# Moving the bound, mirror, statistics and row-number pieces of the even attention steps in a graph-network kernel's tick plan

## The chip, the core and the metric

The kernel runs on one core of a Trainium2 chip. The metric is device time in microseconds (us) of one execution. Three runs of the kernel before gave 1163.94, 1170.53 and 1171.4 us, median 1170.53. One more execution was recorded by the hardware profiler and took 1240.64 us.

The engines are written PE (TensorE, matmuls), DVE (VectorE), ACT (ScalarE), POOL (GpSimd) and SP (SyncE, which issues transfers). Each works through its own list of instructions, and semaphores hold an instruction until what it needs is there.

## What is computed

Sixteen graphs of 1024 nodes with 128 features each, and a 0/1 adjacency matrix per graph. Layer 0 is masked attention, layer 1 a three-stage graph convolution on a thinned ("dilated") adjacency:

```python
h = jnp.maximum(_layernorm(x, axis=-1), 0.0)
# layer 0
v = relu(h @ Wv.T + bv); q = relu(h @ Wq.T + bq); k = relu(h @ Wk.T + bk)
att = softmax((q @ k.T) * mask - NEG * (1.0 - mask))
x = x + relu((att @ v) @ Wo.T + bo)
h = jnp.maximum(_layernorm(x, axis=-1), 0.0)
# layer 1: the pattern is thinned row by row; earlier rows' removals count
def step(carry, n):
    row = carry[n]; num = row.sum()
    sf = where(num > 10, (num + 1) // 2, 1)
    rm = row & (cumsum(row) % sf == 0) & (num > 1)
    carry[n] = row & ~rm; carry[:, n] &= ~rm
adj_d = adj * dilate(adj)
# three times: agg = adj_d @ h / deg; h = bn(relu(normalize(agg @ Wr + h @ Wx + b)))
# then x + concat(h1, h2, h3) @ Wl + bl
```

The adjacency is sparse enough that most rows cannot lose a neighbour. The kernel therefore finds the few rows that can (the "bound"), sorts them, gathers their rows, solves the thinning for them alone, and checks that the input is of the kind that allows this (0/1 entries, symmetric).

## The kernel before

`fast` runs three stages. The first is attention, one step per graph: `step(i)` for i = 0 to 15, and it is there that the change lies. The graph convolution follows in the later part of the program (three passes, with batch norms between them).

**A step and its ticks.** A step has 16 blocks of scores: two groups of 512 queries by eight blocks k of 128 keys. In each block, `scores` issues one matmul of 128 x 512 (L731), whose exponential (ACT, L733) and product with the mask (DVE, L734) are queued one and two ticks later. After that come twice two matmuls of `values` (L747) for the group before. The function `pace` is called three times in a block, once after the scores and once after each half of the values; each call is one **tick**. A step thus has 48 ticks. Everything else that has to be done beside attention is written as generators which yield between pieces, and a plan says at which tick of a step each generator is advanced. Ticks over 47 fall into the next step. Each piece is put on its engines' lists at its tick, in the order of the agenda, so the plan fixes the order of instructions on each engine.

**The pieces that the change touches**, for step i:

- `bound(i)` (`AT_BOUND`), 17 pieces. Piece 0 is `prepare`: the upper triangles of the diagonal blocks `du` (DVE, L210) and two limits (L211, L213). Then for each of eight blocks of rows k two pieces: matmuls into a PSUM buffer `pd` (k times L237 on the comparisons `away` of the blocks before, then one L238 on `du`), and a DVE comparison L240 that reads the `pd` and writes `away[k]`. Block k + 1 needs the comparison of block k.
- `mirrors(i)` (`AT_MIRRORS`), 8 pieces. Piece k transposes k + 1 blocks of the adjacency on PE into a `pd` (L193), and one tick later DVE compares them with the rows (L199).
- `project(i + 1)` (`AT_PROJECT`), the next graph's q, k and v. Its first five pieces are the layer norm's statistics: four DVE statistics (L590), then the last one, with a DVE negation (L593) and a chain of 14 small POOL instructions (L597 to L603). Four pieces of normalising on POOL (L609, which writes `hn`), two of PE transposes (L619) and the matmuls (L710, L718) follow.
- `gather(b)` (`AT_GATHER`), for the two graphs b of a pair, planned in odd steps; many of its ticks are over 47, so they run in the next even step. Its pieces: four of DVE one-hots (L295); PE row numbers into a `pd` (L300); a DVE instruction that reads them (L303); an indirect DMA on POOL (L306) that fetches the rows; a DVE scan over them (L310); the codes (DVE, L313); PE transposes into a `pd` (L317); two ACT evictions (L321); PE matmuls into a `pd` (L325); and DVE reads of these (L328, L330, L331). The buffers `rows` and `left` exist once, so the second graph's L306 waits for the first graph's L313.
- `norms_of_x2(i - 1)` (`AT_NORMS`), the statistics of the finished rows in the same form; its last piece is followed by `store(i - 1)` (eight indirect DMAs from POOL, L565) from tick 75.

All these `pd` are turns of one PSUM buffer name with two buffers; so a matmul of a later piece waits until DVE or ACT has read the piece two turns earlier. In PSUM, the scores have two buffers (`ps`), the values two (`po`), the projection one (`pm`), and the solver one (`pb`).

**The solver.** In steps 5 to 7, 9 to 12 and 13 to 15, `solve` is spread over the ticks as well: small DVE instructions, pairs of DVE masks (L367) and PE matmuls (L399, L400) that need both masks.

**The scheduling is by hand.** The order in the lists is the order in which the code issues; nothing is moved later. In the plan, the first entry of each pair of lists is for even steps and the second for odd ones, except in `AT_GATHER`, where the first is for the pair's even graph and the second for its odd graph. In step 0 every tick t becomes 24 + t // 2.

```python
plan(dil.bound(i), start, late(AT_BOUND[odd]))
plan(dil.mirrors(i), start, late(AT_MIRRORS[odd]))
if i + 1 < B:
    plan(project(i + 1), start, late(AT_PROJECT[odd]))
```

## Time and profile before

| | us |
|---|---|
| median of three runs (1163.94 to 1171.4) | 1170.53 |
| the profiled execution | 1240.64 |
| its span, first to last instruction | 1238.8 |
| its stretch from the start of step 1 to that of step 15 (72.4 to 735.2) | 662.8 |
| mean granted PE clock over the span | 0.946 |

The profile has, for each engine, how long it was busy and in which instructions, named by line, tile and shape; what an engine waited for before an instruction ("idle before <- releaser"); a chain of waits that leads to the last instruction; and tables by stretch of the span, with the clock that was granted to PE. A line of the timeline reads: start in us, duration in us, engine, line, operation, output <- inputs, shape, count, and in brackets the idle time before it with what ended it. Matmul ends in it are modelled, so that neighbouring matmuls overlap by some tenths of a microsecond.

The costliest attention groups, and the DVE groups that stand around the bound:

| group | busy, us | mean of one, ns | idle before |
|---|---|---|---|
| PE L747, values, x2048 | 315.3 | 289 | 0.0 |
| PE L731, scores, x512 | 272.4 | 616 | 0.8 |
| DVE L734, mask product, x256 | 177.9 | 695 | 162.4, mostly for ACT's exponential |
| ACT L733, exponential, x256 | 153.1 | 598 | 120.4, mostly for the scores |
| DVE L310, scan, x16 (median of one) | | 2283 | |
| DVE L313, codes, x16 (median of one) | | 1218 | |
| DVE L590, statistics, x128 (median of one) | | 418 | |
| DVE L240, the bound's comparison, x128 (median of one) | | 152 | |

### The profile page before, as it was taken

How to read it: one execution, taken by the hardware profiler on the slowest of the kernel's cores; microseconds unless marked ns; L12 is line 12 of the kernel's file. 1: busy time of each engine (PE TensorE's matmuls, PEld its weight loads, DVE VectorE, ACT ScalarE, POOL GpSimd, SP SyncE). 2: the span in 40 equal slices, each digit the busy share in tenths (PEclk: the TensorE clock that was granted, in tenths of full speed). 3: DMA queues.
4: the chain of work that ended last, by engine and by line, in shares of the span. 5: the costliest groups of instructions: out<-in, count | busy, mean ns of one | idle time of the engine just before them, and what ended most of it. 6: DMA issues, size and time to landing. Idle time of an engine off the chain costs nothing.

```text
span 1238.8 us, 22489 instructions
## 1 busy us (share of the span) xinstructions
PE 1077.9 (87%) x7731; PEld 832.2 (67%) x7731; DVE 850.6 (69%) x2611; ACT 736.8 (59%) x1772; POOL 566.4 (46%) x1071
## 2 busy tenths in 40 slices
PE   7899998997998999899999898687879988788675
PEld 2566676665676676676666666576769977778565
DVE  6667567578677667777777778678878866555432
ACT  5577787876776777776776652276757722222211
POOL 0220642651733643643634514678601037767552
PEclk8899999999899999999999899999989989889698
DMA  6444345344344344344343321334010037667534
GB/s 210 140 133 137 104 137 153 102 125 148 90 120 135 113 126 144 104 129 137 112 128 90 121 65 37 90 90 119 1 35 1 2 89 224 208 199 205 160 118 129
DMA packets 138589, 145.89 MB, mean 118 GB/s; under 512 B 25952, under 2 KB 114400, under 8 KB 138464
## 3 DMA queue, kind: packets, MB, share of 16 engines
q1 hardware_dynamic: 126432, 112.68, 32.1%
q0 software_dynamic: 12032, 31.67, 7.7%
q8 instruction: 63, 1.03, 0.4%
q14 instruction: 62, 0.51, 0.1%
HBM read 114.76 MB, written 29.56 MB: 116 GB/s over the span
## 4 chain that ended last, share of the span: by engine, by line
PE 59%; DVE 19%; ACT 8%; POOL 4%; issue 4%; another core or an unknown queue 3%; DMA 1%; SPq 0%; DVEq 0%; POOLq 0%; ACTq 0%
PE po L747 13%; PE ps L731 13%; PE pm L710 6%; PE po L1019 5%; DVE e L734 3%; PE pd L193 3%; PE pt L1077 2%; ACT e L733 2%; PE ph L1359 2%; PE ph L1297 2%; POOL hn L609 2%; PE ph L1298 2%; DVE left L310 2%; PE pm L718 1%
## 5 line engine op out<-in xcount | busy, mean ns | idle before, releaser
L747 PEld LDWEIGHTS po<-vw,e 128*128 128x128 f32 x2048 | 278.3, 198 | 62.7 <-issue 62.3
L747 PE MATMUL po<-vw,e 128*128 128x129 f32 x2048 | 315.3, 289 | 0.0
L734 DVE TENSOR_TENSOR e<-e,ab 128x512 f32<-128x512 f32 x256 | 177.9, 695 | 162.4 <-ACT e L733 145.1
L731 PE MATMUL ps<-qT,kT 128*128 128x512 f32 x512 | 272.4, 616 | 0.8 <-ACT e L733 0.8
L733 ACT ACTIVATE e<-ps 128x512 f32<-128x512 f32 x256 | 153.1, 598 | 120.4 <-PE ps L731 86.3
L565 POOL DMA_INDIRECT x_d<-xt,slot x128 | 142.8, 1115 | 40.4 <-issue 33.2
L167 ACT ACTIVATE ab<-st,d_one_k 128x1024 bf16<-128x1024 f32 x128 | 147.1, 1149 | 2.5 <-DMA st<-in_adj_dram 2.4
L184 ACT ACTIVATE junk<-st 128x1024 bf16<-128x1024 f32 x112 | 118.1, 1054 | 0.0
L565 POOL DMA_INDIRECT y_d<-y,nodes x96 | 94.2, 982 | 23.7 <-issue 20.3
L597 POOL TENSOR_SCALAR ln_t<-ln_st 128x8 f32<-128x8 f32 x31 | 7.5, 242 | 207.2 <-DVE ln_st L590 193.2
L306 POOL DMA_INDIRECT rows<-in_adj_dram,row x16 | 18.0, 1124 | 179.5 <-DVE row L303 98.5
L1035 ACT ACTIVATE sq<-po 128x512 f32<-128x512 f32 x48 | 28.6, 598 | 99.9 <-remote 44.7
L731 PEld LDWEIGHTS ps<-qT,kT 128*128 128x128 f32 x512 | 79.5, 195 | 6.6 <-ACT e L733 2.8
L756 ACT ACTIVATE o<-po,recips 128x128 f32<-128x128 f32 x128 | 46.7, 367 | 55.2 <-DVE recips L754 42.7
L1019 PE MATMUL po<-ws,r 128*128 128x128 f32 x512 | 69.9, 280 | 3.3 <-issue 3.3
L1019 PEld LDWEIGHTS po<-ws,r 128*128 128x128 f32 x512 | 66.8, 197 | 5.2 <-issue 4.0
L199 DVE SCALAR_TENSOR_TENSOR junkv<-pd,ab 128x64 bf16<-128x64 int32 (+7 forms) x128 | 57.8, 451 | 17.2 <-PE pd L193 12.3
L609 POOL TENSOR_SCALAR hn<-xt,ln 128x128 f32<-128x128 f32 x120 | 68.8, 588 | 1.6
L1297 PE MATMUL ph<-ws,r 128*128 128x128 f32 x224 | 49.0, 301 | 16.3 <-DVE y L1094 6.2
L609 POOL TENSOR_SCALAR hn<-xt 128x128 f32<-128x128 f32 x112 | 56.3, 516 | 12.7 <-PE pt L619 11.9
L237 PEld LDWEIGHTS <-ab 128*128 128x128 bf16 x448 | 26.6, 98 | 49.7 <-issue 49.4
L1032 ACT ACTIVATE sq<-po 128x128 f32<-128x128 f32 x192 | 51.0, 292 | 10.4 <-PE po L1026 5.7
(341 smaller groups left out, 2439.3 us busy)
## 6 DMA issues: line engine op xcount, KB each, us to landing
st<-in_adj_dram SPq DMA_DIRECT2D x128, 512.0 KB
r<-y_d SPq DMA_DIRECT2D x24, 512.0 KB
xt<-x_d SPq DMA_DIRECT2D x16, 524.0 KB
xt<-in_x_dram SPq DMA_DIRECT2D x16, 512.0 KB
x<-x_d SPq DMA_DIRECT2D x16, 512.0 KB
out_dram<-r SPq DMA_DIRECT2D x12, 512.0 KB
x_d<-xt,slot POOLq DMA_INDIRECT x128
y_d<-y,nodes POOLq DMA_INDIRECT x96
```

The source lines that it names most:

```text
L167: nc.scalar.activation(ab[:, k, :], st, AF.Exp, bias=self.one_k, scale=ONE_K, accum_out=self.deg[:, b, k:k + 1])
L184: nc.scalar.activation(junk(), st, AF.Exp, scale=-ZERO_K, accum_out=zeros)
L199: nc.vector.scalar_tensor_tensor(junk.rearrange("p a b -> p (a b)")[:, :n], pt.rearrange("p a b -> p (a b)").bitcast(I32)[:, :n], 1.0, ab[ ...
L565: d = nc.gpsimd.indirect_dma_start(out=dst, out_offset=bass.IndirectOffsetOnAxis(ap=slots, axis=0), in_=src, in_offset=None)
L609: engine.tensor_scalar(hn[:, k, :], xt[:, k, :D], minus[:, k // 2, k % 2, None], rstd[:, k // 2, k % 2, None], op0=OP.add, op1=OP.mult)
L710: nc.tensor.matmul(pp, w, hT[:, 512 * g:512 * g + 512], start=True, stop=True)
L731: nc.tensor.matmul(p, K[b][:, k * P:(k + 1) * P], Q[b][:, c], start=True, stop=True)
L733: later(1, lambda: nc.scalar.activation(e, p, AF.Exp))
L734: later(2, lambda: nc.vector.tensor_mul(e, e, AB_[b][:, k, c]))
L747: nc.tensor.matmul(po[:, q % 2, :], E[k][:, i * P:(i + 1) * P], V[b][:, k, :], start=(k == 0), stop=(k == NB - 1))
L1019: nc.tensor.matmul(po[:, i, :], hT[:, c:c + P], wxk, start=(i == 3), stop=False)
L1297: nc.tensor.matmul(pz[:, i, :], column(r1, b, g, i), wl0, start=True, stop=False)
```

## The change

Only numbers of the plan change, and with them the order of instructions. In even steps, the bound's two pieces for block k move from ticks 9 + 3k and 10 + 3k to ticks 2 + 5k and 3 + 5k. The mirrors move to 5, 10, 20, 25, 30, 35, 40 and 44. The projection's statistics are taken at ticks 1, 2, 4 and 7 instead of 1, 7, 11 and 12; its fifth piece stays at 13. The odd graph's row numbers (matmul L300 and DVE's L303), which run in the next even step, move from its ticks 6 and 7 to 3 and 4; the even graph's scan stays at tick 7 of that step and its codes at tick 10. Of the norms, the first statistics of even steps moves from 30 to 27; of those planned in odd steps that fall into the next even step, the third statistics moves from tick 10 of it to tick 17, and the last piece from 22 to 24. Odd steps keep the ticks of what runs in them.

```diff
         AT_PROJECT = [m + every(m[4] + 4, 4, 1) + every(m[4] + 12, 10, 3)
-                      for m in ([1, 7, 11, 12, 13], [0, 1, 3, 5, 6])]
+                      for m in ([1, 2, 4, 7, 13], [0, 1, 3, 5, 6])]
         AT_LOAD = every(1, 2 * NB, 3)
-        AT_BOUND = [[0] + [first + 3 * (j // 2) + j % 2 for j in range(2 * NB)] for first in (9, 3)]
-        AT_MIRRORS = ([20, 23, 29, 33, 35, 39, 42, 44], [13, 16, 19, 22, 25, 29, 33, 41])
+        AT_BOUND = [[0] + [first + by * (j // 2) + j % 2 for j in range(2 * NB)] for first, by in ((2, 5), (3, 3))]
+        AT_MIRRORS = ([5, 10, 20, 25, 30, 35, 40, 44], [13, 16, 19, 22, 25, 29, 33, 41])
 
         AT_SORT = [27, 29, 31, 32, 33, 35, 36]
         AT_GATHER = ([37, 38, 39, 40, 43, 44, 47, 55, 58, 63, 64, 65, 69, 70],
-                     [41, 43, 46, 49, 54, 55, 61, 81, 85, 89, 90, 91, 93, 94])
+                     [41, 43, 46, 49, 51, 52, 61, 81, 85, 89, 90, 91, 93, 94])
         LAST_GATHER = [37, 38, 39, 40, 43, 44, 46, 50, 54]
-        AT_NORMS = ([30, 57, 67, 68, 71], [42, 44, 58, 67, 70])
+        AT_NORMS = ([27, 57, 67, 68, 71], [42, 44, 65, 67, 72])
         AT_STORE = every(75, NB, 2)
```

## The prediction

> **What bounds the kernel now.** I read the page's busy shares first, then the chain of waits, then the attention steps one by one, then the queues around the longest wait of a step. On the page TensorE (PE) has most work and the chain runs mainly over it:

> ```profile
> PE 1077.9 (87%) x7731; PEld 832.2 (67%) x7731; DVE 850.6 (69%) x2611; ACT 736.8 (59%) x1772; POOL 566.4 (46%) x1071
> ...
> PE 59%; DVE 19%; ACT 8%; POOL 4%; issue 4%; another core or an unknown queue 3%; DMA 1%; SPq 0%; DVEq 0%; POOLq 0%; ACTq 0%
> ```

> A step begins where VectorE (DVE) builds the upper triangles (L210). These are the even steps 2, 4, 6, 8, 10, 12 and 14 in a table by stretches: the stretch, its length, PE busy, granted clock.

> ```profile
> 115.20:160.70 45.50, 43.09 (x293) 0.96 0.43 138
> 205.20:250.20 45.00, 42.02 (x295) 1.00 0.45 128
> 299.30:349.90 50.60, 44.93 (x317) 0.93 0.39 118
> 398.30:444.00 45.70, 43.28 (x293) 0.96 0.44 133
> 491.30:536.80 45.50, 42.29 (x308) 0.96 0.37 114
> 586.90:633.00 46.10, 43.02 (x299) 0.96 0.43 127
> 682.00:735.20 53.20, 46.19 (x316) 0.90 0.35 105
> ```

> PE is busy 92% of an even step, so a step ends when PE ends it, and PE's idle time and slow clock are the only things to win. Going through PE's timeline, each of these steps has one large gap, and it is always the same instruction: the second matmul of the bound (L237) waits for DVE's comparison L240. The gaps are 2.21, 2.22, 4.06, 2.21, 2.83, 1.79 and 4.06 us, 19.4 in all. Step 4, DVE and then PE, shows why:

> ```profile
> 210.22 2.28 DVE L310 TENSOR_TENSOR_SCAN left<-rows 128x1024 f16<-128x1024 f32 x1
> 212.43 0.13 DVE L303 TENSOR_SCALAR row<-pd 128x1 int32<-128x1 f32 x1
> 212.47 0.41 DVE L590 BATCH_NORM_STATS2 ln_st<-xt 128x6 f32<-128x256 f32 x1
> 212.81 0.67 DVE L734 TENSOR_TENSOR e<-e,ab 128x512 f32<-128x512 f32 x1
> 213.40 1.22 DVE L313 SCALAR_TENSOR_TENSOR left<-rows,left 128x1024 f16<-128x1024 f32 x1
> 214.54 0.42 DVE L590 BATCH_NORM_STATS2 ln_st<-xt 128x6 f32<-128x256 f32 x1
> 214.87 0.14 DVE L240 TENSOR_TENSOR d_away<-pd,d_limits 128x2 bf16<-128x2 f32 x1
> ...
> 211.83 1.02 PE L731 MATMUL ps<-qT,kT 128*128 128x512 f32 x2
> 215.06 0.16 PE L237 MATMUL pd<-d_away,ab 128*128 128x2 bf16 x1 [2.22 <-DVE d_away L240]
> ```

> The comparison is 0.14 us long, but it stands behind the scan and the codes (L310, L313: 3.4 us), row numbers, two statistics and a mask product. PE has nothing else in order, so it stops.

> The gap has a second price. The stretches just behind six of the gaps (all but that of step 4) have the clock at one half; step 4 and step 6 as examples:

> ```profile
> 215.10:218.50 3.40, 3.40 (x32) 1.00 0.66 204
> 309.40:316.10 6.70, 6.06 (x36) 0.50 0.27 78
> ```

> PE was busy 24.2 us in those six stretches (3.30, 6.06, 3.30, 3.00, 3.02, 5.50); at full clock that work takes half, so 12.1 us are lost. Gaps and slow clock, 19.4 + 12.1 = **31.5 us, are the ceiling** of what the even steps can give here.

> [...] Bound, mirrors and gather share two banks (`pd`) here; no run yet shows what a tighter rotation costs.

> **The change part by part.** No instruction is added or removed; built, the two programs have the same order on ACT, POOL and SP. Only PE's and DVE's orders change, in even steps. A block of scores takes 3 ticks and 1.86 us (206.17 to 207.92 and 209.96 to 211.83 in step 4), a tick 0.62 us.

> *Bound from tick 2, five ticks a block; row numbers at 3 and 4; first statistics at 1, 2, 4, 7; mirrors at 5 and 10.* The comparison for block 1 is now at tick 8, right behind the scan of tick 7 and one statistic, and its reader is at tick 12. Step 4 by the durations above. DVE from 206.15: mask product 0.61, one-hot 0.39, two statistics 0.67, residual 0.36, comparison 0, mask product 0.6, row number, statistic 0.34, mirror comparison 0.3, to about 209.6; the next mask product waits for ScalarE's exponential as now and ends near 210.3; scan 2.2, statistic 0.33, comparison 1 near 212.9, seen by PE 0.19 later (214.87 to 215.06 today): 213.1. PE arrives where it arrives now, 211.83 + 1.02 = 212.85, plus what has been put ahead (three mirror transposes at 0.07, one more bound block 0.1): 213.2. The gap goes; I allow 0 to 0.3 us. PE's transposes L317 then come at about 215.3 instead of 216.95, with 0.3 us more work done: **1.9 us a step** in the clean steps 2, 4, 8: 5.7. The clock stretches behind the gaps of 2 and 8 (3.30 busy each) go too: 3.3.

> *What is late next.* ScalarE waits for the reciprocal L754 (214.93, a wait of 2.47 us); it moves to about 215.2, and the exponential behind it frees the scores' buffer near 216.5, wanted at 217.1: covered. POOL: its row gather waits for L313, then it computes the scales and the blocks `hn`; four were done at 223.5 in step 4 and PE's L619 came at 225.62. Now L313 ends 0.3 later and PE comes 1.9 earlier: cover of 2.1 us shrinks to nothing, cost 0 to 0.3 a step. Statistics taken earlier do not help POOL, for the gather stands ahead of them. The final norm, ticks 22 to 24, stands behind `hn` on POOL anyway (POOL went from `hn` at 225.4 straight into it) and the stores begin at tick 27 as before: nothing. The norms' first statistics, moved from tick 30 to 27 and from 10 to 17, cost 0.33 us of DVE each where DVE waits for ScalarE: nothing. Mirrors spread to tick 44: each comparison is 0.2 to 0.7 us in DVE's gaps of 0.4 to 3.4 us after 226: nothing while DVE leads. The second scan (tick 33) now stands ahead of comparison 6 (reader at tick 37, 2.5 us): covered by DVE's lead of about 1 us in step 4.

> *Steps 6 and 14*, where the solver's masks share DVE. DVE is never idle from 299.3 to 309.9, so the order can't win its time. PE reaches the first bound matmul near 299.0, but the triangles and their limits end at 300.1: a new gap of about 1. Comparison 1 costs about 0.9, and the solver's matmul L399, which needs the second mask (done 309.83 now, 0.8 later behind one more statistic, two comparisons and a mirror), about 1.8. Sum 3.7 against 4.06. L399 comes near 310.9 instead of 311.95, and if the three smaller gaps leave the clock alone the step gains 3.4 (1.05, the 0.3 put ahead, and 2.06 of half-clock loss still behind L399), if not 0.4. I take 2.0 each: 4.0. *Steps 10 and 12*, with half of that load: the same walk leaves gaps of about 2.6 in step 10, so mostly the clock (3.0/2 each): 1.5 each, 3.0; ends 0 and 2.5.

> *Step 0*: the four statistics are done about 1.3 us earlier, and PE waits there 2.18 us for POOL's `hn`: 1.0; ends -1 and 2.

> **Sum:** 5.7 + 3.3 + 4.0 + 3.0 + 1.0 = 17.0 us from the profiled execution, 1240.6 to 1223.6 (1.4%). That execution is 70 us above the runs' median of 1170.53, and nothing here shows which part of it is longer, so I carry the share over: 16 us, **1155 us**.

> **Rivals.** (1) *DVE stays the bound and the clock still drops.* For it: 10.6 us of unbroken DVE work in step 6. The loaded steps give nothing, the clean ones 5.7 and half the clock's: gain 7, 1163. (2) *The runs hardly have these gaps*, being shorter than the profile: gain 0 to 4, 1168. Against it: the gap is DVE's own work, not slow transfers. (3) *Slower: two banks tie PE to DVE at more places.* In ticks 2 to 12 PE now takes a bank six times instead of three, each freed by a DVE read. It decides once DVE runs more than about 1.4 us behind at tick 7 (scan 2.2, statistic and comparison 0.5, against 3.1 us to tick 12); the loaded steps do. If clean steps slip too, each gets a further gap of 1 and a clock stretch of 1.7 less what goes now: some +1.6 a step, +11, 1182. (4) That the orders don't move is excluded: the built program has them.

> **Numbers.** Forecast 0.60, (1) 0.19, (2) 0.09, (3) 0.12. About 1% (11.7 us, below 1158.8) is what a measurement here can tell from none. The forecast's own range is 1143 to 1163 (the clock in the loaded steps, 12, and the covers, 4): nine tenths of it is faster, so faster 0.54, same 0.34, slower 0.12. The range 1140 to 1173 holds the ceiling's 31.5 at its lower end and rivals 1 and 2 at its upper.

> **What would show it.** Right: no wait of L237 on L240 above 0.5 us in steps 2, 4, 8, those steps near 42.5 us at clock 1.00, L399 the longest PE wait of steps 6 and 14. Wrong: PE waiting for L240, L303 or L199 at several places in ticks 2 to 12, 0.50 stretches in clean steps, or L619 waiting for POOL by over 0.5 us.

## The result, and the profile after

Six runs of the changed kernel gave a median of 1161.16 us (1159.38 to 1161.68), six of the kernel before 1166.41 us (1161.54 to 1171.4). The ratio is 0.9948, with a 95% interval of 0.9922 to 0.9973: 0.5% faster, some 6 us by the ratio, where 16 were forecast.

The profiled execution of the changed kernel took 1161.53 us (span 1159.7). Its 79 us to the profiled execution of before are not the change: a copy of the changed kernel on another chip, below, has a span of 1241.4. By its time and its mean clock (0.946) the profile before came from such a slower chip, the one after (0.968) from a faster. So spans and odd steps are not compared between these two; the even steps are, since for the changed kernel they come out alike on both kinds of chip (318.4 and 319.0 us in sum, each step counted from one L210 to the next).

The table by stretches for the even steps 2 to 14 of the changed kernel (stretch, length, then PE, its weight loads, DVE, ACT and POOL busy, granted clock, two columns of transfers):

```profile
117.04:160.84 43.80, 41.91 (x293) 29.61 (x292) 28.54 (x80) 34.27 (x68) 23.71 (x45) 1.00 0.38 120
203.64:247.84 44.20, 42.31 (x295) 29.73 (x294) 28.59 (x81) 34.61 (x68) 23.72 (x45) 1.00 0.41 118
293.84:342.34 48.50, 43.90 (x317) 31.36 (x318) 37.78 (x130) 34.70 (x69) 24.26 (x45) 0.96 0.40 121
387.54:431.44 43.90, 42.01 (x293) 29.61 (x292) 28.55 (x80) 34.22 (x68) 23.72 (x45) 1.00 0.41 121
477.44:522.04 44.60, 41.52 (x308) 29.49 (x309) 33.89 (x104) 33.43 (x65) 24.09 (x45) 1.00 0.37 110
567.54:613.44 45.90, 41.89 (x299) 29.35 (x299) 34.98 (x110) 33.85 (x68) 22.40 (x45) 1.00 0.40 117
659.34:706.84 47.50, 43.25 (x315) 31.23 (x316) 37.21 (x128) 34.39 (x67) 24.45 (x45) 0.96 0.39 115
```

Together 318.4 us, against 331.6 before. The columns split the 13.2 us: PE's busy time fell from 304.8 to 296.8 us, by 8.0, and its idle time from 26.8 to 21.6, by 5.2. The instructions are the same, so most of the 8.0 must be the clock's part: five of the seven steps are at 1.00, where only one was, and the two at 0.96 have one stretch of 3.4 us at half clock each.

The idle time fell little. Before, PE's gaps over 0.4 us in the even steps summed to 25.1 us: 19.4 are the large ones at L237, and 2.6 are two at L710 in steps 6 and 14. No profile from a faster chip has a wait at L710 over attention, so these two may be the slower chip's. After, gaps over 0.4 us sum to 19.4 us again, at other lines. PE's waits over attention in the view of waits (who waited for whom, us in total, times, longest):

```profile
PE pd L237 <- DVE d_away L240: 5.1, 14, 1.0
PE pm L619 <- ACT hT L620: 5.0, 4, 1.3
PE pb L400 <- DVE m L367: 3.6, 2, 1.8
PE pd L238 <- DVE d_first L211: 3.2, 4, 0.9
...
PE pm L619 <- POOL ln_t L603: 1.8, 2, 0.9
PE pm L619 <- POOL ln_t L601: 1.5, 1, 1.5
```

No wait of the bound (L237, L238) is longer than 1.05 us now. But L619 is new: 5.0 + 1.8 + 1.5 = 8.3 us, one wait of 0.9 to 1.5 us in each of the seven steps. Step 4, PE's line and then ACT's list up to it (lines left out are marked):

```profile
226.68 0.63 PE L619 MATMUL pm<-identf,hn 128*128 128x128 f32 x4 [1.25 <-ACT hT L620]
...
222.52 0.37 ACT L332 ACTIVATE d_code<-pd,d_used 128x128 f16<-128x128 f32 x1 [1.70 <-DVE recips L754]
222.78 1.05 ACT L184 ACTIVATE junk<-st 128x1024 bf16<-128x1024 f32 x1
...
224.07 0.59 ACT L733 ACTIVATE e<-ps 128x512 f32<-128x512 f32 x1
...
224.80 1.16 ACT L167 ACTIVATE ab<-st,d_one_k 128x1024 bf16<-128x1024 f32 x1
...
225.93 0.61 ACT L620 ACTIVATE hT<-pm 128x512 f32<-128x512 f32 x1
```

The projection has one PSUM buffer `pm`. The second four transposes of L619 need the eviction L620 of the first four. These were done near 223.4 (start 222.83), but L620 stood behind 3.4 us of ACT's own work and, before that, a wait of 1.70 us. Before the change ACT had the same order, and the second four followed without a wait:

```profile
225.62 0.60 PE L619 MATMUL pm<-identf,hn 128*128 128x128 f32 x4
227.23 0.61 ACT L620 ACTIVATE hT<-pm 128x512 f32<-128x512 f32 x1
228.07 0.60 PE L619 MATMUL pm<-identf,hn 128*128 128x128 f32 x4
```

Step 4 begins (L210) at 205.20 in that profile and at 203.71 in the changed kernel's. Counted from there, PE comes to the first four 1.3 us earlier (20.42 and 19.12 us), L620 starts 0.2 us later (22.03 and 22.22), and the second four come 0.1 us later (22.87 and 22.97). The wait has taken back the whole lead that PE had at this place; the 0.8 us by which step 4 is shorter come after it. Three of the seven waits stand under POOL in the view; there too L620 ends just ahead of the matmul (in step 6 at 320.56, with PE's start at 320.71), so the release is put down to ACT here.

### The profile page after: what moved, and what is told of

It is laid out like the page before. It is cut to its first block, busy times and chain, and to the rows that moved or that the text cites. A ratio compares the mean times of both kernels' runs of the same rounds, so it can differ in the third digit from the quotient of the medians.

```text
span 1159.7 us, 22501 instructions
## 1 busy us (share of the span) xinstructions
PE 1048.9 (90%) x7731; PEld 817.1 (70%) x7731; DVE 846.9 (73%) x2611; ACT 734.7 (63%) x1772; POOL 574.7 (50%) x1071
## 4 chain that ended last, share of the span: by engine, by line
PE 53%; DVE 19%; ACT 12%; POOL 9%; issue 3%; DMA 3%; POOLq 0%; DVEq 0%; SPq 0%; ACTq 0%
PE ps L731 12%; PE po L747 11%; PE pm L710 6%; PE po L1019 4%; POOL hn L609 3%; DVE e L734 3%; ACT e L733 3%; PE pt L1077 2%; PE pd L193 2%; ACT ab L167 2%; PE ph L1359 2%; PE pm L718 2%; DVE left L310 2%; ACT junk L184 1%; PE ph L1297 1%
## 5 line engine op out<-in xcount | busy, mean ns | idle before, releaser
L747 PEld LDWEIGHTS po<-vw,e 128*128 128x128 f32 x2048 | 276.6, 194 | 78.4 <-issue 78.2
L747 PE MATMUL po<-vw,e 128*128 128x129 f32 x2048 | 308.1, 283 | 0.0
L734 DVE TENSOR_TENSOR e<-e,ab 128x512 f32<-128x512 f32 x256 | 178.0, 695 | 146.4 <-ACT e L733 145.6
L731 PE MATMUL ps<-qT,kT 128*128 128x512 f32 x512 | 270.2, 611 | 0.8 <-ACT e L733 0.8
L167 ACT ACTIVATE ab<-st,d_one_k 128x1024 bf16<-128x1024 f32 x128 | 146.9, 1148 | 6.6 <-DMA st<-in_adj_dram 6.5
L731 PEld LDWEIGHTS ps<-qT,kT 128*128 128x128 f32 x512 | 78.6, 193 | 7.3 <-issue 2.9
L199 DVE SCALAR_TENSOR_TENSOR junkv<-pd,ab 128x64 bf16<-128x64 int32 (+7 forms) x128 | 57.5, 449 | 12.7 <-PE pd L193 12.5
L237 PEld LDWEIGHTS <-ab 128*128 128x128 bf16 x448 | 26.5, 97 | 46.5 <-issue 46.1
L193 PE MATMUL pd<-d_id,ab 128*128 128x128 bf16 x576 | 53.3, 220 | 0.7 <-DVE junkv L199 0.4
```

The lines of the kernel that those rows point to most:

```text
L167: nc.scalar.activation(ab[:, k, :], st, AF.Exp, bias=self.one_k, scale=ONE_K, accum_out=self.deg[:, b, k:k + 1])
L193: nc.tensor.transpose(pt[:, j, :], ab[:, j, k * P:(k + 1) * P], self.identb)
L199: nc.vector.scalar_tensor_tensor(junk.rearrange("p a b -> p (a b)")[:, :n], pt.rearrange("p a b -> p (a b)").bitcast(I32)[:, :n], 1.0, ab[ ...
L731: nc.tensor.matmul(p, K[b][:, k * P:(k + 1) * P], Q[b][:, c], start=True, stop=True)
L734: later(2, lambda: nc.vector.tensor_mul(e, e, AB_[b][:, k, c]))
L747: nc.tensor.matmul(po[:, q % 2, :], E[k][:, i * P:(i + 1) * P], V[b][:, k, :], start=(k == 0), stop=(k == NB - 1))
```

## Experiments

The ratios below are to runs of the kernel before on the same chip.

**The two kernels unchanged, on slower chips.**

> The kernel before once more, for a second profile of it. The first profiled execution took 1240.6 us, 6% more than the runs, the one of the changed kernel 1161.5 us, as its runs do. Theory A (the gap at L237 is part of every run, and the changed kernel gives most of it back at L619): the new profile has a span near 1165 us, L237 waiting for L240 by 2 to 4 us in each even step as before (18 to 20 us in the seven), odd steps without the 2.8 us waits of L710, and even steps of 44.5 to 46 us. Theory B (these gaps belong to the one slow execution): L237 waits less than 1 us in most even steps and they last about 44 us. Ratio to the kernel before 1.000 within 0.002 under both.

Measured: 1244.34 us, ratio 1.0016 (0.9993 to 1.0039), span 1233.8. The waits at L237 are 2.22, 2.22, 4.07, 2.22, 2.83, 1.80 and 4.07 us: those of the first profile, at most a hundredth apart. They belong to the order and not to one execution. The span near 1165 us was not met, for this chip is a slower one, and the waits of L710 in odd steps came back too, so they are no accident of one execution either. What did differ is the clock: behind the gaps of 2.2 us in steps 2 and 8 it stayed at 1.00 here (0.96 in the first profile); the last section lays the two beside each other. The even steps sum to 331.1 us all the same.

> The changed kernel unchanged, so that its copy and the kernel before are profiled on one chip. Theory A (what the change gains lies in the even steps' bound, 2 to 4 us each, and 0.9 to 1.5 us of it is given back where the second half of the L619 transposes waits for the one pm buffer, which L620 on ScalarE empties): on a chip whose kernel before takes 1243 us the ratio is 0.986 to 0.992, even steps 2 to 14 sum to 320 us against 331, odd steps stay near 329 to 331, L619 waits for L620 by 0.9 to 1.5 us in each even step. Theory B (the chip sets it: where transfers come late the change gains nothing): ratio 0.997 to 1.003, even steps within 3 us of 331.

Measured: 1243.16 us, ratio 0.9895 (0.9839 to 0.9951), even steps 319.0 us, the seven L619 waits again (0.9 to 1.5 us). That is theory A; odd steps summed to 340.6 us and not 329 to 331.

**The bound and mirrors alone.** Of the change, only these lines:

```diff
-        AT_BOUND = [[0] + [first + 3 * (j // 2) + j % 2 for j in range(2 * NB)] for first in (9, 3)]
-        AT_MIRRORS = ([20, 23, 29, 33, 35, 39, 42, 44], ...
+        AT_BOUND = [[0] + [first + by * (j // 2) + j % 2 for j in range(2 * NB)] for first, by in ((2, 5), (3, 3))]
+        AT_MIRRORS = ([5, 10, 20, 25, 30, 35, 40, 44], ...
```

> Only the bound and the mirrors moved; statistics, row numbers and norms as in the kernel before. The row numbers' matmul then takes its PSUM buffer at tick 6 and is read behind the scan at tick 7, while the bound takes its second buffer at tick 7 and the mirror its at tick 10. Theory A with the buffers: the matmul of block 1 of the bound waits for its buffer till L303 has read the row numbers behind the scan, a gap of 1 to 3 us in each even step, so no gain or a loss: 1166 to 1180 us, ratio 1.000 to 1.012. Theory B (the comparison's place alone counts): as the changed kernel, ratio 0.995.

Measured: 1229.9 us, ratio 0.9901 (0.9874 to 0.9928), even steps 321.0 us: in the profile these two lines carry the gain. The large waits at L237 are gone. L619 waits 0.86 to 1.45 us in each even step, and the mirror's L193 waits 1.04 us (1.38 in step 12) for DVE's row number; PE's line in step 4:

```profile
210.12 0.27 PE L193 MATMUL pd<-d_id,ab 128*128 128x128 bf16 x2 [1.04 <-DVE row L303]
```

**Everything else alone.** Statistics, row numbers and norms moved; bound and mirrors as before.

> Only statistics, row numbers and norms moved; bound and mirrors as in the kernel before. One statistic and the row number fewer stand between the scan and the bound's comparison for block 0 (0.4 to 0.8 us). Theory A: the gap at L237 shrinks from 2.2 to about 1.6 us in the clean steps, the end of the step stays L619's or ACT's business: 1162 to 1167 us, ratio 0.997 to 1.001. Theory B: same within 0.002.

Measured: 1235.53 us, ratio 0.9942 (0.9914 to 0.997), with the L237 waits at 2.11, 2.11, 3.71, 2.11, 2.65, 1.47 and 3.71 us and even steps of 331.1 us. The clean steps' gap was expected to shrink to 1.6 us and did not. In the profile's even steps this part gains nothing. The runs show 0.6%, more than either theory allowed, which no line of the profile accounts for; that stays open.

**The bound with the row numbers.** The changed kernel with these two lines as before:

```diff
-                      for m in ([1, 2, 4, 7, 13], [0, 1, 3, 5, 6])]
+                      for m in ([1, 7, 11, 12, 13], [0, 1, 3, 5, 6])]
-        AT_NORMS = ([27, 57, 67, 68, 71], [42, 44, 65, 67, 72])
+        AT_NORMS = ([30, 57, 67, 68, 71], [42, 44, 58, 67, 70])
```

> Of the change, the bound, the mirrors and the row numbers; the project statistics and the norms stand where they stood before. Theory A (the gain is the bound's; statistics and norms bring their lines off the same moment of ScalarE and VectorE, worth up to 0.3 us a step): ratio within 0.003 of that of the bound and mirrors alone (0.990), even steps 319 to 323 us, heavy steps 6 and 14 with PE gaps of about 1 at L238 and 1.8 at L399 or L400. Theory D (the early statistics of the whole change cost VectorE time in ticks 1 to 7 just where the bound's sums now stand, and so part of the gain): this one is faster than the changed kernel by 0.004 or more.

Measured: ratio 0.9919 (0.9897 to 0.9942), even steps 321.8 us. The waits of L193 for L303 are gone, so the row numbers' move is what clears them, and L619 waits as ever. Theory D would have needed a ratio 0.004 below the changed kernel's 0.9895; it came out above it, so the early statistics cost nothing that shows.

**Taking the L619 wait away, first try.** In even steps the second half of L619 and all pieces behind it two ticks later:

```diff
-        AT_PROJECT = [m + every(m[4] + 4, 4, 1) + every(m[4] + 12, 10, 3)
+        AT_PROJECT = [m + every(m[4] + 4, 4, 1) + [m[4] + 12] + every(m[4] + (17 if m[4] == 13 else 15), 9, 3)
```

> The changed kernel, with the second half of the projection's transposes (L619) and all that follows it in the projection two ticks later in even steps. In the changed kernel that second half waits 0.9 to 1.5 us in each of seven even steps (8.4 us in all) for ACT (L620) to free the one buffer pm. Theory A (that wait is where the gain went): the waits of L619 in even steps fall under 0.4 us each and the time falls by 4 to 8 us against the changed kernel: 1153 to 1157 us, ratio to the kernel before 0.988 to 0.992. Theory B (ACT is simply late there): the wait moves to the next matmul of the projection (L710 on L711 or L620) and the time stays at 1161, ratio 0.995.

Measured: ratio 0.9949 (0.9923 to 0.9975), not the 0.988 to 0.992 of theory A. The L619 waits are gone and the even steps sum to 305.2 us, but the odd ones to 349.7. The last two pieces now fall later into the odd step, and the second half of L718 stops for DVE in steps 3 to 13 by 1.1 to 3.6 us. In each of these steps ACT has just waited 1.4 to 3.5 us for an adjacency tile, and L719, which L718 waits for, stands on DVE behind a mask product that waits for ACT; step 5:

```profile
252.68 1.15 ACT L167 ACTIVATE ab<-st,d_one_k 128x1024 bf16<-128x1024 f32 x1 [3.52 <-DMA st<-in_adj_dram]
...
255.78 2.00 PE L718 MATMUL pm<-w_L_gnn_Wo,hn 128*128 128x128 f32 x8 [3.55 <-DVE vw L719]
```

**Second try.** Again two ticks later, but the pieces behind it closer together, so that the last two keep their ticks:

```diff
+        ... + ([25, 30, 33, 35, 38, 41, 43, 46, 49, 52] if m[4] == 13 else every(m[4] + 12, 10, 3))
```

> The changed kernel with the second half of the L619 transposes of even steps two ticks later (tick 30 for 28) and the pieces behind it closer together, so that the last ones keep their ticks 49 and 52. Theory A: the L619 wait on L620 falls from about 1.25 us to below 0.4 us in each of seven even steps, the odd steps do not move: even steps some 6 to 9 us shorter than those of the changed kernel on the same chip, ratio 0.005 to 0.008 lower than its ratio. Theory C (VectorE and ScalarE are late as a whole from tick 15 on, so that TensorE waits at the next piece instead): the wait turns up at another line of even steps, with even steps within 2 us of those of the changed kernel and the same ratio within 0.002.

Measured: ratio 0.9931 (0.9907 to 0.9956). In the even steps theory A is right: no L619 wait, 312.4 us against 319.0 on the same chip. Yet the odd steps lose it, 349.3 against 340.6, and the ratio is no lower than the changed kernel's. At the start of step 3, on ACT, DVE and PE:

```profile
163.01 1.15 ACT L167 ACTIVATE ab<-st,d_one_k 128x1024 bf16<-128x1024 f32 x1 [4.00 <-DMA st<-in_adj_dram]
...
164.76 0.69 DVE L734 TENSOR_TENSOR e<-e,ab 128x512 f32<-128x512 f32 x1 [3.69 <-ACT e L733]
165.37 0.15 DVE L240 TENSOR_TENSOR d_away<-pd,d_limits 128x2 bf16<-128x2 f32 x1
...
165.58 0.16 PE L237 MATMUL pd<-d_away,ab 128*128 128x2 bf16 x1 [2.29 <-DVE d_away L240]
```

Read upwards: PE waits for a comparison, DVE in order for an exponential, ACT in order for an adjacency tile that has not landed. The tile is late because of SP. Just ahead of it in SP's list stands the load of x for the step after next (L685), which needs a buffer that POOL's eight stores are still emptying. SP's longest waits from 140 to 160 us in this kernel:

```profile
SPq L685 <- DMA x_d<-xt,slot: 14.3, 2, 7.7
```

Before the change L685 left at 153.14 us, 7.6 us ahead of the start of step 3 at 160.7; here at 155.67, with that step at 156.7. POOL's chain had not become shorter (from the second row gather of step 2 to the last store 26.7 us before, 29.6 here); only PE's had.

**The bound one tick later**, on top of the second try:

```diff
-        ... for first, by in ((2, 5), (3, 3))]
-        AT_MIRRORS = ([5, 10, 20, ...
+        ... for first, by in ((3, 5), (3, 3))]
+        AT_MIRRORS = ([6, 11, 20, ...
```

> As the one with the second L619 at tick 30, and the even steps' bound from tick 3 instead of 2, its first two mirrors at ticks 6 and 11. Theory A: the first L238 of steps 6, 10, 12 and 14 waits 0.6 to 0.9 us for VectorE's d_first column because the bound starts too soon behind the step's start; one tick is about 0.5 us, so these four waits fall by 0.4 to 0.9 us each, together 2 to 3 us, ratio 0.002 lower. Theory C: the same column is waited for at the following block, nothing is won, and a wait of L237 on L240 of over 0.5 us comes back in steps 6 and 14: ratio equal or up to 0.002 higher.

Measured: ratio 0.99 (0.9838 to 0.9961), even steps 316.8 us against 312.4. The wait moved: in step 6 it is 0.84 us at L300 in place of 0.89 at L238, and L237 waits 0.77 (0.46 without the move). In steps 2, 4 and 8 the mirror's L193 now waits 1.08 us for ACT's L321. Nothing was won in the even steps, as theory C had it; the ratios, 0.9900 and 0.9931, have intervals that overlap.

**The load of x later.** L685 is taken from ahead of the step to its tick 11:

```diff
-            plan(dil.mirrors(i), start, late(AT_MIRRORS[odd]))
+            plan(dil.mirrors(i), start, late(AT_MIRRORS[odd])); plan((load_x(b) for b in range(i + 2, min(i + 3, B))), start, [11])
...
             if i + 2 < B:
-                load_x(i + 2)
+                pass
```

> The changed kernel with one transfer moved: the load of x for the step after next (L685) is issued at tick 11 of a step and not ahead of it, so that SyncE no longer waits there for the x_d scatters to end with the adjacency loads (L166) of the coming step queued behind. Theory E (what the even steps win is in part given back at the start of the next odd step, because GpSimd's chain of row gathers, norms and x_d scatters ends no earlier than before and SyncE holds the adjacency tiles behind it): L167 no longer waits for st by more than 0.5 us near the starts of steps 3, 5, 9 and 11 (0.9 to 2.0 us each in the changed kernel), the odd steps sum to 4 to 10 us less than the 340 of the changed kernel on a chip like this, ratio 0.984 to 0.988. Theory F (those waits are short of the critical path, ScalarE catches up within the step): odd steps within 2 us of 340, ratio within 0.002 of 0.9895.

> The kernel before with the x load at tick 11 and nothing else. Theory E: before, SyncE's wait ended some 9 us ahead of the odd step, L167 waited for st at none of steps 3 to 11 (0.4 us once), so there is nothing to win: ratio 0.998 to 1.002, L237 waits for L240 of 2.2 and 4.1 us as before. Theory G (late x loads cost or win time by themselves, whatever the bound does): ratio below 0.996 or above 1.004.

> Both moves: the second half of L619 at tick 30 with the pieces behind it closer together, and the x load at tick 11. Theory E: without the x load's move the odd steps lost (349 us) what the even steps won (312 us), through 2 to 4 us of ScalarE waiting for st at the start of steps 3, 5, 9 and 11 and L237 behind it; with it the waits of L237 on L240 at the start of odd steps fall below 0.5 us, odd steps to 333 to 340 us, even steps stay at 312 us: ratio 0.978 to 0.985, the best of all. Theory F: the odd steps stay near 349 us and the ratio at 0.993.

The last column is from the other chips above.

| kernel, with the load at tick 11 | ratio (95%) | without it |
|---|---|---|
| before | 1.0009 (0.998 to 1.0039) | 1.0016 |
| changed | 0.9865 (0.9813 to 0.9917) | 0.9895 |
| changed, L619's second half at 30, squeezed | 0.9811 (0.976 to 0.9862) | 0.9931 |

In the two changed kernels ACT shows no wait for a tile from step 2 on. On the kernel before the move does nothing that shows. On the changed kernel it took away ACT's waits of 1.1 to 2.0 us, the ratio of 0.9865 lies in theory E's range and not in theory F's, and the odd steps are 3.9 us shorter (336.7 against 340.6); but the intervals overlap and the chips differ, so whether those waits were covered there stays undecided. With the L619 wait gone the move shows clearly: the ratio falls by 0.012, with intervals that do not meet, and the steps are 310.5 (even) and 340.5 us (odd).

**Both moves again.**

> The changed kernel with both moves (second half of L619 at tick 30, x load at tick 11) once more, in five rounds, to see whether 0.981 holds on whatever chip it meets. Theory E (both moves take away what the change had given back, about 1.2 us at L619 in seven steps and 1 to 2 us at the start of four odd steps): ratio 0.976 to 0.986, outside the interval of the changed kernel's first comparison (0.9922 to 0.9973). Rival (the earlier ratio was a favourable sample): 0.987 to 0.995.

Measured: 1154.38 us (1149.79 to 1155.64), before on this chip 1170.13; ratio 0.9882 (0.9846 to 0.9919). The number lies just inside the rival's range, so 0.981 was not confirmed as a size; but the interval lies just below that of the changed kernel's first comparison (0.9922 to 0.9973). This chip was a fast one, so its profile can be laid beside that of the changed kernel. Even steps 2, 4, 6 and 8 by stretches:

```profile
115.74:157.74 42.00, 41.36 (x292) 29.34 (x291) 28.24 (x81) 33.70 (x68) 24.75 (x45) 1.00 0.45 137
200.94:242.94 42.00, 41.37 (x292) 29.33 (x291) 28.24 (x80) 33.71 (x68) 24.78 (x45) 1.00 0.45 136
289.24:336.14 46.90, 42.48 (x316) 29.81 (x316) 37.25 (x128) 33.87 (x67) 25.50 (x45) 1.00 0.42 124
381.34:423.64 42.30, 41.66 (x293) 29.53 (x292) 28.22 (x79) 33.71 (x68) 24.78 (x45) 1.00 0.46 138
```

The even steps sum to 308.0 us against 318.4, the odd ones to 315.3 against 315.6, and step 15 starts at 696.2 against 706.8. The profiled execution was the fastest of its four (1149.79 us); by the medians, 1154.38 against 1161.16, the two moves are worth 6.8 us.

## Why the prediction was partly right

**The bound's gap** was read rightly. It came back within a hundredth in a second execution, and the two lines of the bound and mirrors alone remove it. In steps 2, 4 and 8 no L237 wait over 0.5 us is left (the longest is 0.21), at clock 1.00.

**The step that failed is “late next”.** The prediction looked for what would stop PE at L619 once it came 1.9 us earlier, checked POOL's `hn`, and put the cost at 0 to 0.3 us a step. It checked ACT only for the scores' buffer. The eviction L620 that frees `pm` was on ACT too, and in step 4 PE came 1.3 us earlier in the step and ACT 0.2 us later. The cost was 0.9 to 1.5 us in all seven steps, 8.3 us, where at most 2.1 had been allowed. So steps 2, 4 and 8, forecast near 42.5 us, took 43.8, 44.2 and 43.9; with that wait removed and the tiles in time they took 42.0, 42.0 and 42.3.

**The loaded steps.** The gaps forecast for step 6 were about 1 at the first L238, 0.9 at comparison 1 and 1.8 at the solver's masks. They measured 0.89, 0.46 and 1.78 us (the last at L400, the pair of L399), and nearly the same in step 14. Steps 6 and 14 gained 2.1 and 5.7 us against 2.0 each; in step 14 the wait of L710, 1.98 us with a stretch at half clock behind it, is part of the 5.7, and the prediction had not counted it. Steps 10 and 12 gained 0.9 and 0.2 against 1.5 each.

**The clock.** Of the 12.1 us lost at half clock, some 3.4 are left (two stretches of 3.4 us, busy throughout, of which half is lost: over steps 1 to 14 of the profile before, the median from the start of one L747 matmul to the next is 214 ns at 0.50 and 114 ns at 1.00). That the clock would stay at 1.00 in the clean steps once their gap was gone was the author's estimate; it held, with 1.00 in steps 2, 4 and 8, while steps 6 and 14 came out at 0.96. PE's busy time, 8.0 us shorter in the even steps, agrees roughly; it is the larger part of the 13.2 us. Between the copies on slower chips, 331.1 and 319.0 us, it is 6.5 of 12.1 us. So in the profiles the change wins more by the clock than by idle time.

**Step 0.** Forecast 1.0 us at POOL's `hn`. That wait was 2.18 us before and 3.65 in its copy, 3.21 and 3.22 in the changed kernel: it varies by more than the term.

**The sum.** For the even steps of the profiled execution 16.0 us were forecast, and the two profiles differ there by 13.2. The missing part is idle time: of the 19.4 us of new gaps, the 8.3 at L619 had been put at 2.1 at most. The runs gained 5.25 us by the medians, less than half of what the even steps of the profiles show. The wait at L619 is in both and cannot explain that difference. A part may be L710: both profiles of the kernel before that show its waits in steps 6 and 14 are from slower chips, the changed kernel has them on neither kind, and with the stretch at half clock they make some 4 us, which a faster chip may never have lost. That is not shown, and the rest stays open too; the ratio on the slower chip, 0.9895, has an interval (0.9839 to 0.9951) that overlaps the first one. The time lies in the range of 1140 to 1173 us, and just inside the forecast case's own, 1143 to 1163, at its slow end; the starting point had moved as well, from 1170.53 us in three runs to 1166.41 in six. That the kernel with both further moves took 1154.4 us, beside the 1155 forecast, is a coincidence: it needed two moves that the forecast did not have.

**Rivals.** (1), 1163 us, is near the number and wrong in its mechanism: the loaded steps did gain. (2), that the runs hardly have these gaps, can't be excluded, for no profile of the kernel before was taken on a faster chip. For the slow clock the runs speak against it: seven runs of the kernel before on the chip of the last experiment had a mean granted clock of 0.957 to 0.966, the six of the changed kernel 0.966 to 0.974. By an estimate from the medians (0.959 and 0.970, twice the missing share times the span) that is about 26 us less at half clock in the whole execution; between the two profiles the even steps alone differ by 24 (30.7 and 6.8). (3), more ties of the two `pd` banks: L193 behind L303 at 1.04 us a step in the bound alone is one, and the row numbers' move takes it away; L193 behind L321 came with the bound a tick later. What took back the lead in the changed kernel was another bank, `pm`.

## What to carry to other kernels

When a wait is taken out of the engine that sets the pace, go to every later buffer that exists once, and compare by how much the pacing engine arrives earlier in the step with how much its releaser does (1.3 us and -0.2 us in step 4 here); the releaser's whole list counts, not only its producer. Then do the same with the transfer queues at the end of the stretch, where an earlier end meets a chain that did not become shorter. One wait can cover the next: the late x load showed nothing on the kernel before, and 0.012 of the ratio behind the other move.

## What was not expected of the hardware

One kernel took 1166 to 1170 us on some chips and 1243 to 1256 on others. In the profiles of the slower chips the second `pm` matmul of L710 waits up to 3.3 us for ACT in odd steps, near ACT waits for an unknown queue, and the part after attention's last step start takes 500 to 519 us; in those of the faster, neither such wait appears and the part takes 452 to 453. Why is open.

```profile
121.59:125.00 3.41, 1.29 (x6) 1.00 0.49 123
125.00:128.41 3.41, 3.32 (x12) 0.50 0.66 204
...
210.33:213.75 3.42, 2.52 (x13) 1.00 0.38 145
213.75:217.16 3.41, 2.10 (x16) 1.00 0.71 172
...
119.53:122.94 3.41, 2.06 (x12) 1.00 0.48 142
122.94:126.36 3.42, 2.55 (x24) 1.00 0.63 192
```

In the first pair, 2.1 us of idle time fell into one stretch. In the second the gap was cut by the point at 213.75, 0.90 and 1.31 us, and in the copy it was divided too, 1.35 and 0.87 us. Over steps 1 to 14 of the first profile and the changed kernel's, PE was at full clock in 365 stretches of the grid. Each of the 8 in which it was idle for more than 1.97 us was followed by one at half clock, and none of the 354 with less than 1.57 us; of the three between, the two of 1.78 us were and the one of 1.85 us was not. So in these two profiles the clock went with how much of a gap fell into one stretch of the grid, and single gaps of 1.25 to 1.26 us, one a step, left steps 2, 4 and 8 of the changed kernel at 1.00. In step 6 the wait of 1.78 us lay in one stretch in the changed kernel (303.44 to 306.85), which had a stretch at half clock behind it. With both moves it runs from 299.07 to 300.85 and had none behind it; by an estimate from the matmuls at half clock in step 14 of that profile (661.6 to 665.0), a point of its grid lies near 299.8, so that the wait is cut there.
